# A pre-activation convolution with five quantised weight sets: weights made row by row, statistics of eight images, a written order and smaller last stores

## The chip, the cores and the metric

The kernel runs on one core of a Trainium2 chip. The metric is the device time of one launch in microseconds (us). A kernel is timed several times in alternation with the kernel before on the same chip, and a ratio is formed from the runs of the same rounds. Every profile is of one run. The span from a run's first to its last instruction is 1.7 to 1.9 us shorter than its reported time.

## The reference, cut to what matters

```python
# x: (160, 128, 32, 32) f32; U: (5, 128*128*9) f32; five weight sets, image i uses set i % 5
beta, alpha = max(U), min(U)                       # over all five sets
s1 = (beta - alpha) / 3.0
v1 = s1 * floor(U / s1)
s2 = s1 / 5.0
v2 = s2 * floor((U - v1) / s2)
w  = (v1 + v2).reshape(128 * 5, 128, 3, 3)
g  = group_norm(x, 32 groups of 4 channels, eps 1e-5)
out = x + conv3x3(g, w of the image's set, padding 1)
```

No weight can be made before the range of *all* of `U` is known, and no image can be convolved before its own mean and variance are known. Everything after that is a 3x3 convolution of 128 to 128 channels, 160 times.

## The kernel before

Each image is normalised on VectorE, split in two fp16 parts (`hi`, `lo`) and convolved on TensorE: 9 taps x 2 parts x 2 halves = 36 matmuls. A weight set is quantised on VectorE in one chain of 17 steps over all nine taps (1152 columns), turned by nine f32 transposes on TensorE and copied to fp16 by ScalarE. Images go in chunks of four: one load, one group of statistics, one store. A scheduler chooses the order on each engine.

```python
# class Steps: the range, then some twenty one-column steps (cut)
for n in range(N_SETS):
    nc.vector.tensor_reduce(ext[:, 0, n : n + 1], us[n], AX.X, ALU.max)
    nc.vector.tensor_reduce(ext[:, 1, n : n + 1], us[n], AX.X, ALU.min, negate=True)
nc.vector.tensor_reduce(ext1, ext, AX.X, ALU.max)
nc.gpsimd.partition_all_reduce(extg, ext1, P, bass_isa.ReduceOp.max)
...
def floor_div(self, k, v, n, t, parts):            # 7 VectorE steps, each uses the one before
    r, nr, hi, lo = parts
    nc.vector.tensor_scalar(n, v, r, ROUND, ALU.mult, ALU.add)
    nc.vector.tensor_scalar_add(n, n, -ROUND)
    nc.vector.scalar_tensor_tensor(t, n, hi, v, ALU.mult, ALU.subtract)
    nc.vector.scalar_tensor_tensor(t, n, lo, t, ALU.mult, ALU.add)
    nc.vector.scalar_tensor_tensor(t, t, nr, n, ALU.mult, ALU.add)
    nc.vector.tensor_tensor(t, t, n, ALU.is_lt)
    nc.vector.tensor_sub(k, n, t)
...
def make_weights(n):                               # 7 + 2 + 7 + 1 = 17 steps
    k1, k2, _ = steps.quantise(qpool, us[n], n)
    nc.vector.scalar_tensor_tensor(k2, k1, 5.0, k2, ALU.mult, ALU.add)
    for t0 in range(0, TAPS, 4):
        ...
        for k in range(cnt):
            nc.tensor.transpose(pt[:, k, :], k3[:, :, t0 + k], ident)
        nc.scalar.copy(wt[:, t0 : t0 + cnt, :], pt[:, :cnt, :])
...
# group_statistics, per chunk: measure four images, then
nc.tensor.matmul(pg[:, 0, :], gavg, mv[:, :, 0], start=True, stop=True)   # mean over a group
...                                                                       # deviations
nc.tensor.matmul(pg[:, 1, :], gavg, dv, start=True, stop=True)            # variance
...
nc.gpsimd.tensor_tensor(rstd, ve, mhalf, ALU.pow)
...
total = N_SETS * n_chunks
xts = {g: load(g) for g in range(min(ahead, total))}
wts = {0: make_weights(0)}
norm = statistics(0, xts[0])
pairs = [split(0, j, xts[0], *norm) for j in range(2)]
for g in range(total):
    for j in range(NB):
        ...                                        # split the image two ahead, convolve, residual
    nc.scalar.dma_start(ov[n, :, c * NB : (c + 1) * NB, :], xt)           # 2 MB
```

## Time and profile before

| | |
|---|---|
| time | 1316.07 us median (1315.16 to 1316.87) |
| profiled span | 1314.3 us |
| first convolution starts | 59.06 us |
| last residual starts | 1303.81 us |
| from there to the end of the span | 10.5 us |

Read it as a start, a steady part and a tail. Until 59 us VectorE works and TensorE waits. Then TensorE should be the limit. The stretches show how nearly it is; each line is a window of 50 us with the busy time of TensorE, its weight loads, VectorE, ScalarE and GpSimd, then the granted clock (the share of its full clock that TensorE was given), the DMA share and the rate.

```profile
100.00:150.00 50.00, 48.83 (x237) 23.12 (x235) 48.06 (x66) 8.18 (x10) 3.68 (x2) 1.00 0.34 129
150.00:200.00 50.00, 48.58 (x233) 22.56 (x231) 48.86 (x64) 5.11 (x6) 1.57 (x1) 1.00 0.34 130
```

VectorE is as full as TensorE here (48 of 50 us) and TensorE loses over a microsecond in each window.

### The profile page before, as it was taken

The numbers are of one execution on the slowest core, as the hardware profiler recorded it, in microseconds if no ns is written. First come the engines' busy times: TensorE is split into PE (matmuls) and PEld (weight loads), VectorE is DVE, ScalarE is ACT, GpSimd is POOL, SyncE is SP. The second block draws the span as 40 slices with busy tenths as digits, with TensorE's granted clock in tenths as the row PEclk, the third lists the DMA queues.
The fourth block names the chain that finished last, engine by engine and source line by source line (L and its number), as shares of the span: only waits on it lengthen the run. The fifth ranks groups of instructions, "written<-read, shape, count | busy, mean of one in ns | idle before, by whom it ended". The sixth has DMA issues, their size and how long they took to land.

```text
span 1314.3 us, 13910 instructions
## 1 busy us (share of the span) xinstructions
PE 1243.5 (95%) x5965; PEld 585.9 (45%) x5965; DVE 853.1 (65%) x1317; ACT 168.0 (13%) x176; POOL 47.6 (4%) x51
## 2 busy tenths in 40 slices
PE   0399999999999999999999999999999999999996
PEld 0144444444444444444444444444444444444443
DVE  7999996566697666656555565656666665565441
ACT  0111111111102111111111111111111111111110
POOL 0000000000000000000000000000000000000000
PEclk9999999999999999999999999999999999999999
DMA  8013333343333333333334433434333333333221
GB/s 345 0 43 130 126 150 131 145 157 129 145 128 129 128 128 128 129 128 129 128 139 154 153 133 144 157 114 160 128 129 128 128 128 129 128 128 150 90 81 67
DMA packets 43030, 171.69 MB, mean 131 GB/s; under 512 B 1360, under 2 KB 1360, under 8 KB 42960
## 3 DMA queue, kind: packets, MB, share of 16 engines
q1 hardware_dynamic: 21120, 83.89, 17.2%
q10 hardware_dynamic: 21840, 86.84, 16.5%
q8 instruction: 48, 0.79, 0.2%
q14 instruction: 22, 0.18, 0.0%
HBM read 86.84 MB, written 83.89 MB: 130 GB/s over the span
## 4 chain that ended last, share of the span: by engine, by line
PE 82%; DVE 15%; DMA 1%; POOL 1%; issue 0%; ACTq 0%; ACT 0%; POOLq 0%
PE pc L319 81%; DVE st L135 2%; DVE xt L329 2%; DVE lo L300 2%; DVE z L293 1%; DMA u<-in_L_conv_U_dram 1%; DVE tt L89 1%; DVE k L93 1%; DVE tt L91 1%; DVE tt L90 1%; DVE tt L92 1%; POOL rstd L150 1%; PE pg L146 0%; DVE nn L88 0%; DVE nn L87 0%; DVE k L269 0%
## 5 line engine op out<-in xcount | busy, mean ns | idle before, releaser
L319 PEld LDWEIGHTS <-wt 128*128 128x128 f16 x5760 | 565.5, 99 | 636.7 <-issue 2.4
L319 PE MATMUL pc<-lo,wt 128*128 128x496 f16 (+3 forms) x2880 | 846.3, 376 | 0.0
L319 PE MATMUL pc<-hi,wt 128*128 128x496 f16 (+3 forms) x2880 | 846.2, 376 | 0.0
L329 DVE SCALAR_TENSOR_TENSOR xt<-pc,s2z,xt 128x1024 f32<-128x1024 f32 x160 | 204.4, 1278 | 362.0 <-PE pc L319 362.0
L299 ACT CAST hi<-z 128x1024 f16<-128x1024 f32 x160 | 159.7, 1043 | 1066.4 <-DVE z L293 1066.4
L135 DVE BATCH_NORM_STATS2 st<-xt 128x6 f32<-128x512 f32 x320 | 200.6, 665 | 0.0
L300 DVE TENSOR_TENSOR lo<-z,hi 128x1024 f16<-128x1024 f32 x160 | 188.6, 1219 | 15.8 <-ACT hi L299 15.8
L293 DVE TENSOR_SCALAR z<-xt,gm,rstd 128x1024 f32<-128x1024 f32 x160 | 122.8, 808 | 1.2
L150 POOL TENSOR_TENSOR rstd<-ve,mhalf 128x4 f32<-128x4 f32 x40 | 45.3, 1132 | 1186.3 <-DVE ve L148 1186.3
L139 PE MATMUL pg<-mv,gavg 128*128 128x4 f32 x80 | 11.5, 215 | 33.1 <-DVE mv L136 33.1
L152 DVE TENSOR_SCALAR rstd<-rstd 128x4 f32<-128x4 f32 x40 | 6.8, 170 | 43.5 <-POOL rstd L150 43.5
L139 PEld LDWEIGHTS pg<-mv,gavg 128*128 128x128 f32 x80 | 15.4, 194 | 38.2 <-issue 33.1
L136 DVE BATCH_NORM_AGGREGATE mv<-st 128x2 f32<-128x12 f32 x160 | 31.7, 198 | 1.1
L276 PE MATMUL pt<-ident,k 128*128 128x128 f32 x45 | 9.5, 326 | 17.6 <-DVE k L269 15.5
L146 PE MATMUL pg<-dv,gavg 128*128 128x4 f32 x80 | 13.7, 242 | 9.5 <-DVE dv L145 9.5
L146 PEld LDWEIGHTS pg<-dv,gavg 128*128 128x128 f32 x80 | 12.2, 191 | 20.8 <-DVE dv L145 20.7
L148 DVE TENSOR_SCALAR ve<-pg 128x4 f32<-128x4 f32 x40 | 6.4, 161 | 16.2 <-PE pg L146 16.2
L276 PEld LDWEIGHTS pt<-ident,k 128*128 128x128 f32 x45 | 7.0, 199 | 21.7 <-DVE k L269 15.6
L92 DVE TENSOR_TENSOR tt<-tt,nn 128x1152 f32<-128x1152 f32 x10 | 13.5, 1353 | 0.1
L93 DVE TENSOR_TENSOR k<-nn,tt 128x1152 f32<-128x1152 f32 x10 | 13.4, 1341 | 0.1
L39 DVE TENSOR_REDUCE ext<-u 128x1 f32<-128x1152 f32 x5 | 6.8, 1353 | 8.0 <-DMA u<-in_L_conv_U_dram 7.9
L277 ACT CAST wt<-pt 128x512 f16<-128x512 f32 (+1 forms) x15 | 7.2, 478 | 23.1 <-PE pt L276 23.1
(51 smaller groups left out, 114.8 us busy)
## 6 DMA issues: line engine op xcount, KB each, us to landing
xt<-in_x_dram SPq DMA_DIRECT2D x40, 2048.0 KB, 7.7
out_dram<-xt ACTq DMA_DIRECT2D x40, 2048.0 KB, 6.6
u<-in_L_conv_U_dram ACTq DMA_DIRECT2D x5, 576.0 KB, 11.0
```

Source lines behind the costliest of these rows:

```text
L92: nc.vector.tensor_tensor(t, t, n, ALU.is_lt)
L93: nc.vector.tensor_sub(k, n, t)
L135: nc.vector.bn_stats(st[:, h, :], image[:, h * half : (h + 1) * half])
L136: nc.vector.bn_aggr(mv[:, j, :], st)
L139: nc.tensor.matmul(pg[:, 0, :], gavg, mv[:, :, 0], start=True, stop=True)
L146: nc.tensor.matmul(pg[:, 1, :], gavg, dv, start=True, stop=True)
L150: nc.gpsimd.tensor_tensor(rstd, ve, mhalf, ALU.pow)
L293: nc.vector.tensor_scalar(z, xt[:, j, :], gm[:, j : j + 1], rstd[:, j : j + 1], ALU.subtract, ALU.mult)
L299: nc.scalar.copy(hi_flat, z)
L300: nc.vector.tensor_sub(lo_flat, z, hi_flat)
L319: nc.tensor.matmul(pc[:, h, :].rearrange("p (h w) -> p h w", w=W)[:, r0 - h * HROWS : r1 - h * HROWS, c0:c1], wt[:, tap, :], pair[part][:, ...
L329: nc.vector.scalar_tensor_tensor(xj, pc, steps.s2z, xj, ALU.mult, ALU.add)
```

## The change

The intent is to let the first convolution start with a third of a weight set, to take small work out of TensorE's stream, and to shorten the last store.

- Weights are made in three rows of three taps (384 columns). The first three images are convolved row by row, interleaved with the making of set 0.
- The loads of `U` go first, on two queues; the largest value over partitions comes from two transposes and a matmul instead of a GpSimd all-reduce.
- The weights' integers are written as fp16, so the transposes are fp16, three to a PSUM tile.
- Statistics are taken for 2, 2, 4, 4, 4 and then 8 images at a time.
- The order on each engine is the written one; no scheduler.
- The last four images are stored singly, the very last in two halves.

```diff
-        nc.gpsimd.partition_all_reduce(extg, ext1, P, bass_isa.ReduceOp.max)
+        for k in range(2):
+            nc.tensor.transpose(rows[:, k, :], ext1[:, k : k + 1], ident)
+        nc.vector.tensor_reduce(top, rows, AX.X, ALU.max)
+        nc.tensor.matmul(spread, ones, top, start=True, stop=True)
...
+    def make_row(self, n, row):
+        m = self.qpool.tile([P, P, ROW], MM, tag="m", name=f"m{n}_{row}")
+        un = self.us[n][:, :, ROW * row : ROW * row + ROW]
+        yield from self.steps.quantise(self.qpool, un, f"{n}_{row}", combine)
+        for k in range(ROW):
+            nc.tensor.transpose(pt[:, k, :], m[:, :, k], self.ident)
+        nc.scalar.copy(wt, pt)
...
+        cuts = [0, 2, 4, 8, 12, *range(16, self.imgs + 1, 8)]
...
+        self.xpool = pool("x", 7)
...
+        halves = [slice(0, 1), slice(1, 2)] if i == self.imgs - 1 else [slice(0, 2)]
+        for h in halves:
+            self.nc.vector.scalar_tensor_tensor(
+                xj[:, h], pc[:, h], self.steps.s2z, xj[:, h], ALU.mult, ALU.add
+            )
+            if i >= self.imgs - NB:
+                self.nc.scalar.dma_start(to[:, h], xj[:, h])
...
+        run(row)                       # row 1 of set 0 is done
+        self.remainder(0)
+        self.remainder(1)
+        self.conv(0, 0)
+        self.conv(1, 0)
+        row = self.make_row(0, 0)
+        self.measure(2)
+        self.measure(3)
+        self.stats[1].means()
...                                    # row 0, image 2 normalised
+        self.conv(2, 0)
+        for i in range(self.FIRST):
+            self.conv(i, 1)
+        row = self.make_row(0, 2)
...                                    # row 2, image 3 normalised
+        for i in range(4, 8):
+            self.measure(i)
+        for i in range(self.imgs):
+            for st in ready:
+                st.means()
+            for st in middle:
+                st.variances()
+            self.normalise(i + self.LEAD)
+            if i < self.FIRST:
+                self.conv(i, 2)
...                                    # else all rows of image i
+            self.residual(i - 1)
+            self.remainder(i + self.LEAD)
...                                    # scales, deviations, one or two measurements
+            if later is not None:
+                take(later, 4)         # four steps of the next set's rows
```

## The prediction

> **What bounds the kernel now.** I read the page first, then the chain that ended last, then the timeline of the first 60 us and of the last 12.
>
> From the page, the busy shares and the slices (each digit is tenths of a slice of 32.9 us):
>
> ```profile
> PE 1243.5 (95%) x5965; PEld 585.9 (45%) x5965; DVE 853.1 (65%) x1317; ACT 168.0 (13%) x176; POOL 47.6 (4%) x51
> ...
> PE   0399999999999999999999999999999999999996
> ...
> DVE  7999996566697666656555565656666665565441
> ```
>
> TensorE is full from the third slice to the end and nearly idle in the first one and a half. There VectorE is the busy one. So there are two limits, in sequence: VectorE until the first convolution, TensorE after it.
>
> From the chain in order of time (start, length, what), one steady chunk of four images, one chunk with the weights of the next set in it, and the last stretch:
>
> ```profile
> 820.08 28.38 PE pc L319 x134
> 848.58 2.14 PE pc L319 x10
> 850.88 13.14 PE pc L319 x62
> 866.93 13.54 PE pc L319 x64
> 880.59 2.14 PE pc L319 x10
> 882.89 28.38 PE pc L319 x134
> ...
> 1252.53 51.26 PE pc L319 x242
> ```
>
> The last line gives the pace: 51.26/242 = 0.2118 us per matmul, so an image of 36 matmuls is 7.62 us and 160 images (5760) are 1219.5 us. The change leaves this work alone. From 820.08 to 850.88 is 30.80 us for 144 matmuls, which is 0.30 us over their 30.50: the two f32 statistics matmuls of a chunk. From 850.88 to 882.89 is 32.01, 1.21 us more: nine f32 weight transposes, 0.134 each.
>
> From the timeline, the start and the end (start, length, engine, line, operation):
>
> ```profile
> 6.72 1.35 DVE L39 TENSOR_REDUCE ext<-u 128x1 f32<-128x1152 f32 x1 [6.72 <-DMA u<-in_L_conv_U_dram]
> ...
> 19.69 1.34 DVE L40 TENSOR_REDUCE ext<-u 128x1 f32<-128x1152 f32 x1
> ...
> 53.78 1.36 DVE L269 SCALAR_TENSOR_TENSOR k<-k,k 128x1152 f32<-128x1152 f32 x1
> ...
> 59.06 1.06 PE L319 MATMUL pc<-hi,wt 128*128 128x512 f16 x2
> 59.49 0.15 PEld L319 LDWEIGHTS <-wt 128*128 128x128 f16 x1 [0.28 <-issue]
> 59.54 1.24 DVE L135 BATCH_NORM_STATS2 st<-xt 128x6 f32<-128x512 f32 x2
> 59.54 1.04 ACT L299 CAST hi<-z 128x1024 f16<-128x1024 f32 x1
> 59.91 1.06 PE L319 MATMUL pc<-lo,wt 128*128 128x512 f16 x2
> ...
> 1303.81 1.28 DVE L329 SCALAR_TENSOR_TENSOR xt<-pc,s2z,xt 128x1024 f32<-128x1024 f32 x1 [6.34 <-PE pc L319]
> 1305.12 0.38 ACTq L355 DMA_DIRECT2D out_dram<-xt  x1
> ```
>
> The first convolution waits 59 us for VectorE: range, then all nine taps of set 0, with statistics of three chunks mixed in. The end is a 2 MB store from 1305.1 to the end of the span at 1314.3.
>
> Ledger of the 1314.3: 59.1 start + 1219.5 convolutions + 39 x 0.30 = 11.7 statistics + 4 x 1.21 = 4.8 transposes + about 1.8 slow first matmuls (below) + 10.7 tail (1303.6 to 1314.3) = 1307.6. The remaining 6.7 are PE idle: the windows of 50 us between 100 and 250 and between 350 and 400 show 48.6 to 49.1 busy instead of 50, and less before that.
>
> [...] 1152 elements take 0.750 us for the tensor_scalar by a constant (L88) and 1.353 for the tensor_tensor (L92). [...] 1152 f32 elements at 0.96 per ns are 1.200 us, so L92 has 0.153 fixed and L89 to L91 (1.41) have 0.205; and independent neighbours start about 0.08 us before the former's end. [...] L92 follows L91 (ended 102.77) at 102.80, L93 follows L92 (ended 104.16) at 104.19; a dependent step costs its full length plus 0.03. [...] matmuls 0.42 us apart from 59.06 to 62.4, then 0.21; about 1.8 us lost.
>
> **The change part by part.**
>
> *Three rows of taps.* Seventeen VectorE steps per set become 17 steps per row on 384 elements, 51 per set. Length of a step = fixed part + a third of the stream: L89/90/91 0.605 (0.205 + 0.400), L92 0.553, L93 0.541, L87 0.413 (0.213 + 0.200), L88 0.350, so one floor division is 3.67; two of them, plus 0.414, 0.541 and 0.557 for L104, L105 and L269, are 8.86 us. The steps form a strict chain and the written order keeps them adjacent, where the old schedule put independent work between: 17 x 0.035 more, 9.45 us a row. Three rows cost 28 us against 20.5 for a set before. So the total to the last row grows; only the first row comes sooner.
>
> *Range and loads.* The u loads go first on two queues. At the 410 GB/s of the slices, two of 0.59 MB share the rate and land together near 6.3; the ten reductions then run without the waits at 9.75, 12.83 and 18.42: 10 x 1.27 from 6.3 = 19.0 (before 21.0). Then, in the written order: largest over partitions by transposes, two images' statistics beside it, and 21 one-column steps, chained at about 0.19 each, 3.4 us together: row 1 starts at about 25.7.
>
> *The start, followed on VectorE in written order.* Row 1 with two normalisations (0.73 each) and the small steps ends at 36.8. Three transposes and an ACT copy take about 1.15: **first convolution at about 38.0** (before 59.1). 24 matmuls at 0.2118 + 1.8 slow = until 44.9. VectorE meanwhile does two remainders (2.3) and two measurements (1.43 each) and the head of row 0, and at 42.6 waits for the mean of images 2 and 3, which the written order of PE puts behind those 24 matmuls: 45.3, 2.7 us lost. Row 0 with normalise and remainder of image 2 ends at 56.3. The transposes of row 0 stand ahead of the convolution of image 2, so PE idles from 45 to 56.4; then 48 matmuls, slow at first again, until 68.8. Row 2 with image 3 ends at 67.2, four measurements (5.7) at 72.9. The mean of images 4 to 7 stands on PE ahead of the third row of image 0: **third row from about 73.2**, maybe 1 us of slow clock after 4 us of idling.
>
> *After that* TensorE should never wait. VectorE needs per image 0.73 + 1.20 + 1.14 + 1.43 = 4.5, with four weight steps 6.8 and a second measurement 6.0, all below 7.62, and each product is made one image ahead. So from 73.2: +1.0 clock, 5688 matmuls (5760 less 72 done) x 0.2118 = 1204.7, statistics of 20 groups instead of 38 chunks 20 x 0.30 + one = 6.2, 36 fp16 transposes at an estimated 0.08 = 3.0 (0.134 in f32). PE ends at about 1288.1, before 1303.6.
>
> *Tail.* Half a residual is 1.28 - 0.53 = 0.75, then a store of 256 KB: 0.9 us from issue to moving data and 0.65 moving, instead of 5.2 for 2 MB; what follows the last byte was about 3.1 (1311.2 to 1314.3). 1288.1 + 0.3 + 0.75 + 0.9 + 0.65 + 3.1 = **span 1293.8**, 20.5 less. Before, reported time was 2 over the span: **1296**.
>
> The sum by parts: start and three-row interleave about -7 (73.2 + 1 less the 15.2 of work already done there is 59.0, and the old start is 59.1 plus 1.8 slow plus about 6 of later idling), statistics -5.5, transposes -1.8, tail -5.
>
> **The rivals.**
>
> *A. The first convolution is what counts.* TensorE starts 21 us earlier; if the two idle stretches of the start were filled, 21 + 6 + 12 of the other terms would give about 1278. For: the first row needs a third of the weights. Against: six row convolutions hold only 15 us of work while VectorE has 30 us more of rows and statistics ahead, and PE is in order. It is VectorE's sum that sets the third row.
>
> *B. VectorE's short steps are cheaper than I think.* If a row takes 7.2 us (no gaps, 0.08 overlap), three rows give back 6 us: 1290, right at the threshold of 2%. For: fixed parts are inferred from one length. Against: L92 to L93 above.
>
> *C. A new wait in the steady part*: the written order cannot slip work past a stalled instruction. If each set's 13 images with four weight steps lose 0.5 us, four sets add 26 us and the gain is gone. Against: 6.8 is below 7.62 with an image of lead. GpSimd's power (1.1 to 2.2 us) now sits ahead of one normalisation per group, also with slack.
>
> *D. Statistics and stores were hidden.* Against: the 0.30 stands in TensorE's own stream, and after 1303.8 nothing runs beside the store.
>
> **Range and chances.** Centre 1296. Row cost and semaphore gaps are good to 4 us, the clock to 1.5, transposes to 1.5; unforeseen waits push only upward. Range 1290 to 1303. Over 2% faster means below 1290.1; for that B or part of A must hold: 0.14. Slower by 2% needs C several times over: 0.01.
>
> **What would show it.** In the changed profile: first convolution near 38; a PE idle stretch of about 11 us before the row-0 transposes and one of 4 before the mean of images 4 to 7; row chains of about 9.5 us net; third row at 73; from there no PE idle and 7.62 us per image; last matmul near 1288; last store to span end near 5. Wrong if row steps are much below 0.55 us, if TensorE shows waits at the images with weight steps, or if the tail after the last byte differs.

What the traces and runs show for three things that the prediction uses:

- *0.96 columns per ns.* In the kernel before, an f32 tensor_tensor took 1.353 us for 1152 columns (L92) and 0.162 for 4 (L143): 0.96 columns per ns. In the changed kernel 384 columns took 0.551, which gives 0.96 again. Of the other steps, those of L89 to L91 of the kernel before went from 1.41 to 0.605 (0.95 columns per ns), those of L87 from 0.81 to 0.41 (1.9).
- *The order on TensorE.* A mean that waited held up the matmuls written behind it: in the changed kernel the third row started at 73.96, in e2, where it no longer stands behind that mean, at 69.75.
- *Slow matmuls after idling.* In the changed kernel the granted clock was 0.52 from 56.93 to 59.4, behind the wait of 9.89, and 0.50 from 73.96 to 78.94, behind that of 4.79. The 1 us for the third row was the estimate; 2.8 were measured.

## The result, and the profile after

The changed kernel takes **1295.74 us** in the median (1294.93 to 1296.91, four runs) against 1316.07 for the kernel before in the same rounds. The ratio is **0.9846**, 95% interval 0.9829 to 0.9864. A ratio is the mean time of one kernel's runs over the mean of the other's of the same rounds, so it is not quite the ratio of the medians. It is 1.5% faster. The prediction of 1296 was right. The profile shown here is of the slowest of the four runs (1296.91, span 1295.2); the spans of the others were 1293.2 to 1294.1.

The page of the changed kernel, the same rows as were shown of the kernel before and the clock beside them:

```profile
PE 1238.0 (96%) x5901; PEld 580.1 (45%) x5901; DVE 883.0 (68%) x1367; ACT 174.6 (13%) x177; POOL 43.4 (3%) x57
...
PE   0589999999999999999999999999999999999997
...
DVE  7886788855667887656688866657887566555441
...
PEclk9889999999999999999999999999999999999999
```

TensorE has work in the second slice (5 instead of 3) but is not full in the second and third, where the granted clock also drops to 8. VectorE does more work than before (883 us against 853): the same columns cut in three cost more time (a tensor_tensor of 1152 columns took 1.353 us, three of 384 take 3 x 0.551 = 1.653).

The timeline of the start and of the end (start, length, engine, line, operation, and in brackets what ended the idle time before it):

```profile
6.01 1.35 DVE L323 TENSOR_REDUCE ext<-u 128x1 f32<-128x1152 f32 x1 [5.09 <-DMA u<-in_L_conv_U_dram]
...
17.36 1.34 DVE L324 TENSOR_REDUCE ext<-u 128x1 f32<-128x1152 f32 x1
...
25.48 0.41 DVE L85 TENSOR_SCALAR nn<-u,s1r 128x384 f32<-128x384 f32 x1
...
36.24 0.56 DVE L358 SCALAR_TENSOR_TENSOR m<-k,k 128x384 f16<-128x384 f32 x1
...
37.93 1.03 PE L416 MATMUL pc<-hi,wt 128*128 128x512 f16 x2 [0.57 <-ACT wt L366]
...
45.56 0.16 DVE L164 COPY gm<-pg 128x2 f32<-128x2 f32 x1 [2.98 <-PE pg L156]
...
56.63 0.50 PE L364 MATMUL pt<-ident,m 128*128 128x128 f16 x3 [9.89 <-DVE m L358]
...
73.37 0.59 PE L156 MATMUL pg<-mv,gavg 128*128 128x4 f32 x2 [4.79 <-DVE mv L150]
...
1288.65 1.41 DVE L431 SCALAR_TENSOR_TENSOR xt<-pc,s2z,xt 128x512 f32<-128x512 f32 x2 [6.34 <-PE pc L416]
```

The first convolution starts at 37.93, 21 us earlier than before. Then TensorE stops twice for VectorE: 9.89 us for row 0, and 4.79 us for the four measurements behind row 2. The 2.98 us of the sixth line are VectorE itself standing still, because the mean of images 2 and 3 is behind 24 matmuls in TensorE's order.

The chain from there (start, length, what) and two of the 50 us windows, with the columns of the two lines of before:

```profile
73.96 4.98 PE pc L416 x12
...
79.16 13.04 PE pc L416 x60
...
1204.78 83.85 PE pc L416 x396
```

```profile
100.00:150.00 50.00, 50.00 (x241) 23.40 (x240) 35.74 (x57) 6.27 (x6) 2.54 (x4) 1.00 0.33 127
150.00:200.00 50.00, 50.00 (x243) 23.60 (x242) 42.03 (x70) 7.11 (x8) 1.91 (x2) 1.00 0.44 168
```

The first twelve matmuls of the third row take 4.98 us where twelve take 2.54 at full clock: after the wait of 4.79 the granted clock is low (0.50 from 73.96 to 78.94). From about 100 us TensorE is busy for the whole of each window. At the end the pace is 83.85/396 = 0.2117 us per matmul, the same as before.

Where the gain is: the spans differ by 19.1 us (1314.3 less 1295.2). The last residual starts 15.2 us earlier, and from there to the end are 6.55 us instead of 10.5, so 3.9 come from the tail. By the medians the gain is 20.3. All outputs are right.

### The profile page after: what moved, and what is told of

Same layout as the page of the kernel before. It is cut to its first block, busy times and chain, and to the rows that moved or that the text cites. A ratio compares the mean times of both kernels' runs of the same rounds, so it can differ in the third digit from the quotient of the medians.

```text
span 1295.2 us, 13840 instructions
## 1 busy us (share of the span) xinstructions
PE 1238.0 (96%) x5901; PEld 580.1 (45%) x5901; DVE 883.0 (68%) x1367; ACT 174.6 (13%) x177; POOL 43.4 (3%) x57
## 4 chain that ended last, share of the span: by engine, by line
PE 94%; DVE 5%; DMA 0%; issue 0%; ACT 0%; DVEq 0%
PE pc L416 94%; DVE st L149 1%; DVE ext L323 0%; DVE ext L324 0%; DMA u<-in_L_conv_U_dram 0%; DVE tt L88 0%; DVE tt L89 0%; DVE tt L87 0%; DVE tt L90 0%; DVE k L91 0%; PE pg L156 0%; DVE z L384 0%; PE pg L171 0%; PE pt L364 0%; DVE lo L398 0%; DVE nn L85 0%
## 5 line engine op out<-in xcount | busy, mean ns | idle before, releaser
L431 DVE SCALAR_TENSOR_TENSOR xt<-pc,s2z,xt 128x1024 f32<-128x1024 f32 (+1 forms) x161 | 205.5, 1277 | 370.4 <-PE pc L416 370.4
L392 ACT CAST hi<-z 128x1024 f16<-128x1024 f32 x160 | 167.2, 1045 | 984.0 <-DVE z L384 948.2
L178 POOL TENSOR_TENSOR rstd<-ve,mhalf 128x8 f32<-128x8 f32 (+2 forms) x23 | 35.1, 1527 | 1163.0 <-DVE ve L176 1163.0
L366 ACT COPY wt<-pt 128x384 f16<-128x384 f16 x15 | 7.2, 478 | 102.1 <-DMA out_dram<-xt 59.4
L337 PE MATMUL rows<-ident,ext 128*1 128x128 f32 x2 | 0.6, 394 | 19.1 <-DVE ext L328 19.1
L90 DVE TENSOR_TENSOR tt<-tt,nn 128x384 f32<-128x384 f32 x30 | 16.5, 551 | 0.9
L91 DVE TENSOR_TENSOR k<-nn,tt 128x384 f32<-128x384 f32 x30 | 16.3, 544 | 0.7
L364 PEld LDWEIGHTS <-m 128*128 128x128 f16 x45 | 3.9, 106 | 22.2 <-DVE m L358 19.3
L156 PEld LDWEIGHTS pg<-mv,gavg 128*128 128x128 f32 x46 | 9.0, 202 | 8.6 <-DVE mv L150 5.0
L156 PE MATMUL pg<-mv,gavg 128*128 128x8 f32 (+2 forms) x46 | 7.1, 226 | 5.6 <-DVE mv L150 4.8
L171 PE MATMUL pg<-dv,gavg 128*128 128x8 f32 (+2 forms) x46 | 7.3, 231 | 5.0 <-DVE dv L168 5.0
L86 DVE TENSOR_SCALAR nn<-nn 128x384 f32<-128x384 f32 x30 | 10.6, 352 | 0.8
```

The source lines that it names most:

```text
L90: yield nc.vector.tensor_tensor(t, t, n, ALU.is_lt)
L91: yield nc.vector.tensor_sub(k, n, t)
L156: self.nc.tensor.matmul(self.pg[:, 0, :], self.gavg, self.mv[:, :, 0], start=True, stop=True)
L171: self.nc.tensor.matmul(self.pg[:, 1, :], self.gavg, self.dv, start=True, stop=True)
L178: nc.gpsimd.tensor_tensor(self.rstd, ve, self.mhalf[:, : self.nb], ALU.pow)
L392: nc.scalar.copy(hi.rearrange("p h w -> p (h w)"), z)
```

## The experiments

Each is the changed kernel with one edit, unless another base is named. My theory was that set 0's chain on VectorE decides the start, and that the early first convolution buys little. The rival was that the early start is the gain. The small terms of the sum were measured one at a time. "Last residual" is the start of the last residual on VectorE, and separates the tail from the rest. Span and last residual are of the one profiled run, so a difference of a microsecond or so between two rows may be the run's; the medians and ratios don't have that weakness, but the experiments were timed in other rounds than the changed kernel (e1 to e4 on one chip, the rest on another), each against the kernel before on its own chip.

| run | median, us | ratio to before (95%) | span, us | last residual, us |
|---|---|---|---|---|
| changed kernel | 1295.74 | 0.9846 (0.9829 to 0.9864) | 1295.2 | 1288.65 |
| e1_nine | 1295.42 | 0.9841 (0.9827 to 0.9854) | 1293.7 | 1286.97 |
| e2_mean_behind | 1293.76 | 0.9830 (0.9816 to 0.9843) | 1292.3 | 1285.82 |
| e3_mean_between | 1293.62 | 0.9827 (0.9813 to 0.9840) | 1291.9 | 1285.23 |
| e4_both | 1293.76 | 0.9829 (0.9816 to 0.9843) | 1290.1 | 1283.10 |
| e5_groups4 | 1301.48 | 0.9893 (0.9878 to 0.9908) | 1299.4 | 1292.57 |
| e6_one_store | 1299.97 | 0.9882 (0.9867 to 0.9897) | 1298.2 | 1287.60 |
| e7_f32_transposes | 1298.33 | 0.9862 (0.9846 to 0.9877) | 1297.2 | 1290.49 |
| e8_nine_order | 1288.97 | 0.9798 (0.9785 to 0.9812) | 1286.8 | 1280.66 |
| e9_means_late | 1293.68 | 0.9830 (0.9816 to 0.9843) | 1292.1 | 1285.51 |
| e10_six_three | 1289.12 | 0.9797 (0.9783 to 0.9810) | 1287.5 | 1280.69 |
| e11_six_three_early | 1284.33 | 0.9763 (0.9749 to 0.9776) | 1282.6 | 1276.43 |
| e12_all_reduce | 1295.40 | 0.9845 (0.9833 to 0.9857) | 1294.2 | 1287.70 |

### e1_nine: set 0 in one chain of nine taps, no interleave

```diff
-        row = self.make_row(0, 1)
+        row = self.make_nine()         # 17 steps on 1152 columns, then three turns of three taps
...
+        self.turn(1)
         self.conv(0, 0)
-        self.conv(1, 0)
-        row = self.make_row(0, 0)
         self.measure(2)
         self.measure(3)
+        self.turn(0)
+        self.conv(0, 1)
...                                    # also: one buffer of x fewer (6), to make room
```

> Changed kernel with one thing altered: the nine taps of the first set are made in one chain of 17 steps on 1152 elements (20.5 us of steps, as before the change) instead of three chains on 384 (9.45 us each), and images are then convolved whole, one after the other; the written order is kept otherwise (x buffers 6 instead of 7 for room). Theory (the sum of VectorE's work up to the last row sets the start, and three rows make that sum larger): first convolution near 50 instead of 37.9, but no idling of TensorE after it except about 1.3 us for two weight copies; counted as if all work began at once, 53.5 instead of 61.5; span about 1287 against 1295.2, so 8 us faster. Rival A (the early first convolution is what gained): slower by the 12 us by which the first convolution comes later, span about 1307.

The first convolution started at 49.67, 12 us later than in the changed kernel, and the kernel was still not slower: the ratio is 0.9841 against 0.9846, and the profiled span 1.5 us shorter. So the early first convolution is not what counts. The 8 us that I expected did not come, because a new wait took their place. The first convolution in the chain of this run, and the wait in its timeline:

```profile
49.67 4.94 PE pc L441 x12
```

```profile
70.67 0.39 PE L174 MATMUL pg<-dv,gavg 128*128 128x4 f32 x2 [3.52 <-DVE dv L171]
```

The deviations of images 4 to 7 stood behind two remainders, a measurement and a residual on VectorE; TensorE waited 3.52 us for them and then ran slowly (82 matmuls in 19.04 us, 1.7 over their 17.37; the granted clock from 70 to 80 was 0.83).

### e8_nine_order: e1 with those deviations moved ahead

```diff
         self.normalise(3)
+        self.conv(1, 0)
+        self.stats[2].means()
+        self.stats[2].deviations()
         self.remainder(2)
...
-                self.conv(1, 0)
-                self.stats[2].means()
-                self.stats[2].deviations()
```

> The kernel of e1 with two small steps moved: on VectorE the deviations of images 4 to 7 stand ahead of the remainders of images 2 and 3, and on TensorE their mean stands behind the first row of image 1 and their variance behind its second. Theory (e1's promised gain was lost in the 3.5 us wait of that variance for VectorE and in the slow clock after it, about 1.6): neither is seen, TensorE never idles over 0.7 us after its first convolution, last residual near 1281.9 instead of 1287.0, span about 1288.5, so 5 us faster than e1 and 6.7 than the changed kernel; then three rows are not what the gain rests on. Rival (one chain of nine taps is as slow as three rows for another reason): under 2 us against e1.

A few small instructions in another place are worth 6.9 us of span against e1 (6.5 by the medians). From the chain of this run:

```profile
49.55 4.22 PE pc L441 x12
...
66.43 17.77 PE pc L441 x84
```

TensorE starts 11.6 us later than in the changed kernel and finishes 8.0 us earlier; the medians differ by 6.8, and the ratio of 0.9798 lies outside the changed kernel's interval. The granted clock over the run is 0.999 instead of 0.992. After 49.55 there is no wait over 0.7 us, and one slow stretch is seen and not three: the first twelve matmuls took 4.22 us, the next twelve 2.69, and the 84 from 66.43 on 17.77 (0.2115 each). **The three rows of set 0 are not needed for the gain.** One chain in a good order is faster than three rows in the order chosen, and than the other four orders of three rows below (e2, e3, e4, e9: 1293.6 to 1293.8).

### e2_mean_behind: the mean of images 4 to 7 behind the third row of images 0 and 1

```diff
+            if i > 0:
+                for st in ready:
+                    st.means()
...
+                if i == 0:
+                    self.conv(0, 2)
+                    self.conv(1, 2)
+                    self.stats[2].means()
```

> Changed kernel with the mean matmul of images 4 to 7 moved on TensorE behind the third rows of images 0 and 1, its variance matmul behind the third row of image 2. Theory (that matmul, waiting for VectorE's four measurements, is what holds the third row at 73.96): the third row starts when its weights are copied, near 69, TensorE idles under 1 us there and keeps its full clock; 5.0 of waiting and 2.6 of slow clock go, span about 1287.6, 7.6 us faster. Rival (the weights of the third row, or the clock by itself, hold it): under 2 us.

The third row came at 69.75, right behind the copy of its weights, and at full clock (24 matmuls in 5.20 us; the granted clock from 70 to 80 was 1.00). So the wait of 4.79 before the third row was due to the mean's place in TensorE's order and not to row 2. But the span fell by 2.9 only (the median by 2.0). The chain shows the third row, the timeline what came instead:

```profile
69.75 5.20 PE pc L416 x24
```

```profile
89.09 0.39 PE L156 MATMUL pg<-mv,gavg 128*128 128x4 f32 x2 [2.79 <-DVE mv L150]
```

VectorE is behind by then: the measurement of image 11 ends at 89.04, and the next mean (images 8 to 11) waits for it. TensorE arrives earlier and waits later.

### e3_mean_between: the mean of images 2 and 3 between the convolutions of images 0 and 1

```diff
         self.conv(0, 0)
-        self.conv(1, 0)
         row = self.make_row(0, 0)
         self.measure(2)
         self.measure(3)
         self.stats[1].means()
+        self.conv(1, 0)
```

> Changed kernel with the mean matmul of images 2 and 3 moved on TensorE from behind the first rows of images 0 and 1 to between them. Theory (VectorE's chain sets the third row, so its 2.98 us wait for that mean is lost in full): the wait goes, the third row starts near 71.0 instead of 73.96, span about 1292, 3 us faster. Rival (TensorE's own idling before the row-0 transposes absorbs it, as the convolutions ahead are just as long): the transposes come earlier, but the span does not move by over 1 us.

VectorE no longer stands still, and everything after moves by that: the third row comes at 71.07 instead of 73.96 (chain below), and the last residual is 3.4 us earlier (the medians differ by 2.1). This is the cleanest of the runs of the start: the standstill of VectorE was worth about its 2.98 us, as long as VectorE sets the start.

```profile
70.49 0.58 PE pg L156 x2
71.07 4.92 PE pc L416 x12
```

### e4_both: e2 and e3 together

> Both moves together. Theory: they add, as one is on VectorE's chain and the other takes TensorE off the end of it: third row near 66, span about 1284.6, 10.6 us faster than the changed kernel, and over 2% faster than the kernel before. Rival (one hides the other): the larger of the two alone, about 7.6.

The third row came at 67.05. The wait for image 11 stood at 86.38 with 2.8 us again. The profiled run was 1.8 us shorter than e3's, but it was one of the two fast ones of five: these two took 1291.86 and 1290.91 us at a granted clock of 0.995 over the run, the other three 1293.76 to 1295.44 at 0.993, so that the median is that of e2 and e3. As a timing the run is inconclusive. The scatter goes with the granted clock; in which stretch it was lost is not known, as only one run has a trace.

### e9_means_late: e4 with every later mean behind the second row of its image

```diff
-            if i > 0:
-                for st in ready:
-                    st.means()
...
                 for r in range(len(self.ROWS)):
+                    if r == 2:
+                        for st in ready:
+                            st.means()
                     self.conv(i, r)
```

> The kernel of e4 with the mean matmul of every later group moved on TensorE from ahead of an image's first row to behind its second. Theory (in e2 and e4 the gain was partly turned into the next such wait, 2.79 us for the measurement of image 11): that wait goes and none comes in its place, last residual near 1280.3 instead of 1283.1, span about 1287.3. Rival (VectorE is behind as a whole, so that the wait only moves to the product of image 6 or 8): TensorE shows a wait of 2 us or more for a product, span near 1290.

A miss. The wait for image 11 was gone, but the median is that of e4 (1293.68 and 1293.76), and against e4's profile the last residual came 2.4 us *later*. The timeline at a later weight set:

```profile
213.35 0.17 DVE L164 COPY gm<-pg 128x8 f32<-128x8 f32 x1 [2.81 <-PE pg L156]
...
216.63 0.35 PE L364 MATMUL pt<-ident,m 128*128 128x128 f16 x3 [0.79 <-DVE m L358]
```

Now VectorE waits 2.81 us for the late mean, its next weight row is late by that, and TensorE waits 0.79 us for it. This happens once per later set, four times, 3.2 us. The early place of the mean is right in the steady part and wrong in the start.

### e10_six_three: set 0 as six taps, then three

```diff
-        cuts = [0, 2, 4, 8, 12, *range(16, self.imgs + 1, 8)]
+        cuts = [0, 3, 6, 9, 12, *range(16, self.imgs + 1, 8)]
...
-        row = self.make_row(0, 1)
+        row = self.make_six()
...
+        self.turn(1)
         self.conv(0, 0)
+        self.turn(0)
         self.conv(1, 0)
+        self.conv(0, 1)
+        self.conv(1, 1)
+        row = self.make_row(0, 2)
...                                    # means late everywhere, as in e9; 6 buffers of x
```

> Start rebuilt by the theory: six taps of the first set in one chain of 768 elements, then three; images 0 to 2 share one group of statistics; means of groups stand behind the second row of an image. The chains sum to about 15.3 + 9.45 = 24.8 us instead of 28.4, the first convolution comes near 45.8, and TensorE always has rows of three images to do until the last weights are there. Theory (VectorE's sum, and what stands in front of what, set the start): no wait of TensorE over 1 us after the first convolution; all work as if begun at 48 instead of 61.5; last residual near 1276, span about 1282, 2.6% faster than the kernel before. Rival (something else binds in the first 100 us, as VectorE's backlog over images 3 to 8): waits of several us at images 3 to 6, span 1286 or more.

Convolution from 45.14, third row at 63.63; then the wait of e9 again, from the waits of this run (waited for: us in total, times, longest):

```profile
PE pt L368 <- DVE m L362: 3.2, 4, 0.8
```

The start did what the theory said (after the first convolution TensorE waited for nothing else by more than 1.0 us), but the span missed the 1282 by 5.5 us. Most of that is this loss in the steady part, as e11 shows.

### e11_six_three_early: e10 with the means ahead of the image from image 12 on

```diff
+            if i >= 12:
+                for st in ready:
+                    st.means()
...
-                    if r == 2:
+                    if r == 2 and i < 12:
```

> The kernel of e10 with one thing put back: from image 12 on, the mean matmul of a group stands ahead of an image's first row again, as in the changed kernel; behind the second row only before that. Theory (e10's start was 4.3 us ahead of e8's at image 3, and was given back later: with the mean behind the second row VectorE waits 2.4 to 2.8 us for it in an image with weight steps, and the row's transposes then wait for VectorE, 0.8 us in each of four sets): no transpose waits after the start, last residual near 1276.5 instead of 1280.7, span near 1283. Rival (the loss lies in the start, as in the pairs of matmuls or in the smaller groups): no change over 1 us.

As expected. No transpose waits in the steady part any more, and the last residual is 4.3 us earlier than in e10 (0.3 of it is the pace of the first twelve matmuls, 4.98 us instead of 5.30).

```profile
1276.43 1.41 DVE L457 SCALAR_TENSOR_TENSOR xt<-pc,s2z,xt 128x512 f32<-128x512 f32 x2 [6.34 <-PE pc L442]
```

This is the best version: **1284.33 us**, ratio to before 0.9763, so 2.4% faster than before and some 0.9% faster than the changed kernel (1284.33/1295.74 = 0.991, from medians of different rounds).

### e5_groups4: statistics of four images throughout

```diff
-        cuts = [0, 2, 4, 8, 12, *range(16, self.imgs + 1, 8)]
+        cuts = [0, 2, 4, 8, 12, *range(16, self.imgs + 1, 4)]
```

> Changed kernel with groups of four images throughout instead of eight after image 16: 18 groups more, each with two f32 matmuls on TensorE at 0.12 each, as the changed trace shows. Theory: steady part 18 x 0.24 = 4.3 us longer, last residual near 1293, span about 1299.5. Rival (the pairs of matmuls fill gaps that are there anyway): no change over 1 us.

As expected. Reckoned from the convolution of image 4 on, 18 more groups cost 5.4 us: 0.30 for a pair of statistics matmuls. The pair is not hidden.

### e6_one_store: one store for the last four images

```diff
-            if i >= self.imgs - NB:
-                to = self.ov[n, :, b, :].rearrange("p (h f) -> p h f", h=2)
-                self.nc.scalar.dma_start(to[:, h], xj[:, h])
-        if i < self.imgs - NB and i % NB == NB - 1:
+        if i % NB == NB - 1:
```

> Changed kernel with one store of 2 MB for the last four images, as before the change; the last image's residual stays in two halves. Theory: from the end of the last residual to the end of the span 9.2 us as before the change, instead of 5.1, so the span is about 4.1 longer, 1299.3. Rival (the end of the span is set by something else after the last matmul): no change over 1 us.

The timeline at the end of this run:

```profile
1287.60 1.41 DVE L431 SCALAR_TENSOR_TENSOR xt<-pc,s2z,xt 128x512 f32<-128x512 f32 x2 [6.33 <-PE pc L416]
1289.03 0.38 ACTq L435 DMA_DIRECT2D out_dram<-xt  x1
```

From the residual's end (1289.01) to the end of the span are 9.2 us, against 5.1 in the changed kernel. The single stores are worth 4.1 us. The last residual is 1.05 us earlier than in the changed kernel for a reason outside the edit: the twelve first matmuls of the third row took 4.03 us here and 4.98 there.

### e7_f32_transposes: weights kept in f32 until they are turned

```diff
-        m = self.qpool.tile([P, P, ROW], MM, tag="m", name=f"m{n}_{row}")
+        m = self.qpool.tile([P, P, ROW], F32, tag="m", name=f"m{n}_{row}")
...
-            nc.tensor.transpose(pt[:, k, :], m[:, :, k], self.ident)
+            nc.tensor.transpose(pt[:, k, :], m[:, :, k], self.ident32)
```

> Changed kernel with the weights' transposes in f32 again (45, of which 36 in the steady part). Theory: 0.134 us each as before the change instead of 0.055, so 36 x 0.079 = 2.8 us longer, span about 1298. Rival (f32 transposes are hidden in weight loads): no change over 1 us.

The chain of this run, at the first row of a later set:

```profile
192.04 0.34 PE pt L364 x3
192.39 22.86 PE pc L416 x108
```

Three transposes take 0.34 us of the stream; in the changed kernel the same gap is 0.16 (192.24 less 192.08, the end of the stretch before). From the convolution of image 4 on the run is 1.87 us longer, 0.052 for each of the 36 transposes (the medians differ by 2.6), less than the 2.8 expected: I had estimated from the 0.134 of the kernel before, and three f32 transposes to a tile cost only 0.115 each.

### e12_all_reduce: the range over partitions on GpSimd, as before

```diff
-        for k in range(2):
-            nc.tensor.transpose(rows[:, k, :], ext1[:, k : k + 1], ident)
+        nc.gpsimd.partition_all_reduce(extg, ext1, P, bass_isa.ReduceOp.max)
...
```

> Changed kernel with the range over partitions by GpSimd's all-reduce again, in place of transposes, a reduction and a spreading matmul. Theory (the range over partitions is hidden behind two measurements of 1.4 us each, which are due anyway, whichever way it is made): third row moves by under 1 us, earlier by about 0.5 for the small VectorE steps that go; span 1294 to 1296. Rival (the all-reduce costs more than the 0.5 us between its input and its first use in the trace of before): over 2 us slower.

Row 1 started at 24.87 instead of 25.48, as expected, but the first convolution did not (37.99 against 37.93). The timeline of this run:

```profile
19.02 0.37 POOL L336 PARTITION_ALL_REDUCE extg<-ext  x1 [15.68 <-DVE ext L328]
...
27.43 0.15 DVE L176 TENSOR_SCALAR ve<-pg 128x2 f32<-128x2 f32 x1
...
30.32 0.73 POOL L178 TENSOR_TENSOR rstd<-ve,mhalf 128x2 f32<-128x2 f32 x1 [10.92 <-DVE v L102]
...
31.44 0.81 DVE L375 TENSOR_SCALAR z<-xt,gm,rstd 128x1024 f32<-128x1024 f32 x1 [0.60 <-POOL rstd L180]
```

GpSimd starts its power at 30.32, 10.9 us after the end of the all-reduce (19.39), though its input was written at 27.58; in the changed kernel it starts 0.16 us after its input. The normalisation then waits 0.60 us for it, just what the all-reduce had saved. (The releaser named on the power is not one of its inputs.) What held the power for 2.74 us is not shown. In the kernel before, the power came 18 us after the all-reduce, and 0.17 us after its input (40.63 against 40.46). The change of method for the range was thus about neutral.

## Why the prediction was right, point by point

**The start.** The VectorE sequence was followed instruction by instruction and held to within a microsecond: reductions from 6.01 (predicted 6.3), row 1 from 25.48 (25.7) to 36.80 (36.8), first convolution at 37.93 (38.0), row 0 ended at 56.57 (56.3), row 2 at 67.70 (67.2), third row at 73.96 (73.2). Steps of 384 columns took 0.62, 0.56, 0.56, 0.41 and 0.36 us (predicted 0.605, 0.553, 0.541, 0.413 and 0.350); from 1152 to 384 columns the comparison went from 1.36 to 0.56, which is the 0.96 columns per ns that the prediction reckoned with. One sum in the prediction doesn't come out: 21 one-column steps at 0.19 are 4.0 us and not 3.4. Measured were 3.28 (22.20 to 25.48), as steps that don't use each other's result start 0.06 to 0.08 us apart, those that do 0.18 to 0.20. The standstill of VectorE was 2.98 us (2.7); e3 shows that it was real and worth its length.

**The clock at the third row** was too small: predicted 1.0 us, measured 2.8 in the profiled run (twelve matmuls 4.98 instead of 2.54, the next sixty 13.04 instead of 12.7). The slow stretches of this profile lasted 4.2, 2.5 and 5.6 us (37.93 to 42.2, 56.93 to 59.4, 73.8 to 79.4); the granted clock was 0.52 in the second and 0.50 in the third, while in the first the record shows 1.00, though the matmuls there started 0.42 us apart. Part of the 2.8 is the run's: in the profiles of e5, e6 and e12, whose order of the start is the same, the loss was 1.3 to 1.4 us, in e7 2.6.

**The steady part.** From about 100 us TensorE did not wait, and an image took 7.64 us, as written. The transposes cost 0.053 us each, not the estimated 0.08: 1.9 us in all instead of 3.0. An added statistics pair cost 0.30 in e5, as read; in the changed kernel's own chain a pair takes 0.25 (eight images from 284.61 to 345.84 are 61.23 us, their 288 matmuls at 0.2117 are 60.98), 1.0 less over the 20 groups. With 1.8 lost to the clock, 0.8 to the later third row, and 1.1 gained in the transposes and 1.0 in the pairs, the last matmul ended at 1288.6 instead of 1288.1.

**The tail.** Predicted 5.7 us from the last matmul to the end of the span, measured 6.6. The prediction took only the last half residual to follow the last matmul. Both halves did, 1.41 us instead of 0.75. In the built program the first half waits for a count of TensorE that is 36 above that of the image before, so for all matmuls of the last image, and the second half has no wait of its own; in the trace the last matmul ends at 1288.62 and the first half starts at 1288.65. Halving the residual gained nothing, although the first half's matmuls had been done 3.8 us earlier. Nor does halving the store show a gain: each half took 2.9 us from issue to landing, an undivided store of 512 KB just before 2.6. What e6 shows is the worth of single stores against one of 2 MB; the last one of 2 MB took 7.5 from issue to landing in the kernel before. A version with a wait for each half was not built.

**From span to time** the prediction added 2.2 us; it was 1.7. The span of the profiled run is 1.4 us over the predicted 1293.8, of which 0.5 are the last matmul and 0.9 the tail; but this was the slowest of four runs, and the spans near the median were 1294.0 and 1294.1. So 1296.0 against 1295.74 is a fair hit and in part a lucky one: the clock and the tail were too small, the transposes and the added 2.2 too large.

**The sum by parts.** The tail is worth 3.9 (e6: 4.1; predicted 5). There are 17 pairs of statistics fewer (23 groups instead of 40), at 0.30 about 5.1, and some 6 with the remaining pairs at 0.25 (predicted 5.5). The 36 later transposes went from 0.134 to 0.053, 2.9 (predicted 1.8; of it 1.9 is the fp16, by e7). Of the 15.2 us by which the last residual came earlier, that leaves 6 to 7 for the start and all else (predicted 7), as a remainder and not as a measurement of its own. The prediction's own four parts add to 19.3, not to the 20.5 by which it shortened the span; its terms for the start give 7.9 rather than 7.

**The rivals.** A fell: in e1 and e8 the first convolution starts 12 us later, and the kernel is as fast or faster. B fell: the steps had their length. C did not occur in the changed kernel; e9 and e10 show that it was near, as one late mean per set brings it back (3.2 us). D fell by e5 and e6. What the prediction didn't see is that the sum of VectorE's work, which it called the limit of the start, could simply be made smaller: it reckons that three rows cost 28 us against 20.5, but took this as the price of an early start, which was itself worth little.

**What stays open.** The two queues for the loads of `U` (the ten reductions end at 18.7 us instead of 21.0) and the written order as such were not taken back alone; what they are worth is within the remainder. In which stretch the runs of e4 lose different amounts of clock, and whether that is all of its scatter of 4.5 us; how much of e8's and e11's gain is the shorter chain and how much the order around it, as both were changed together.

## What to carry to other kernels

When a long preparation on one engine feeds a saturated one, splitting the preparation buys only what the consumer can do with the parts; count the consumer's work in hand against the producer's work still ahead, and prefer the split (here six taps and three) that adds least to the producer's work (here each further step of a set cost 0.15 to 0.2 us, by the times at 1152 and 384 columns). With a written order, look at each small cross-engine round trip (a mean, a variance) in both places: too early in a queue stalls that engine for its producer (4.79 us before the third row of the changed kernel), too late stalls the producer's next work (2.81 us in e9). At the end of a kernel ask what is still to be moved after the last result (here 2 MB in one store cost 4.1 us more than single stores), and when an instruction is split, check in the built program that the first part doesn't wait for the whole.
